# Filler products in six waits of TensorE: an attention front and two local-attention layers on one core

## Chip, core and metric

The kernel runs on one core of one Trainium2 chip. The metric is the device time of one execution in microseconds (us). A core has five engines, each with its own instruction queue, which it works off in order: TensorE (PE; its weight loads are shown apart as PEld), VectorE (DVE), ScalarE (ACT), GpSimd (POOL) and SyncE (SP), which here does nothing but issue DMA transfers. [...]

## Reference

Eight sequences of 1024 tokens, 256 wide, float32. First an attention with one head of 64 and a residual, then a normalisation over the width:

```
z = softmax(q k' * 64**-0.5 + causal mask) v;   z = z wo + bo
x = layernorm(x + z)
```

Then two layers (DEPTH = 2) of this, where `shift` moves the second half of the width by one token:

```
q, k, v = split(shift(x) wqkv)           # 8 heads of 64
q, k = rotary(l2norm(q) * q_scale), rotary(l2norm(k) * k_scale)
x = x + local_attention(q, k, v) wo      # blocks of 128 tokens: own and previous block
h = layernorm(shift(x)) * ln_g + ln_b
a, g = split(h w1 + b1)                  # 682 columns each
x = x + (a * gelu(g)) w2 + b2
```

The output is layernorm(x0 + x), with x0 the output of the front.

## The kernel before

**Products.** An operand that needs full precision is split into a high and a low half of type float32r (`halves`, L88; `split_weight`, L184), and a product takes three passes: high by high, high by low, low by high (`products`, L93, and `passes`, L135). Turning a block of 128 by 128 is also an instruction of TensorE, with an identity matrix as one operand. Every group of products writes a tile of PSUM; the tile is read by ScalarE and VectorE, and when they are done the buffer goes to a later tile. The front has 4 PSUM buffers "ps" of 128x512 and two of twice the size, "sc"; the layers have 4 and 4.

**Front** (`fronts`, L217). For each sequence b, `stages(b)` (L273) gives the steps: "load" of half a sequence; "turn" (transposes `xp` of x and split into `f_xT`; then GpSimd adds bo to x); "qkv" (`project`, L299: products `pq` of 128x512 for q and v together, `pk` for k; ScalarE and VectorE write q and k with the high half on partitions 0 to 63 and the low half on 64 to 127, and two DMA transfers, L322, make the swapped copy of q); "back" (transposes of v, `pv`); "sc" for a block of 128 queries (scores, minimum L354/L356, exponent L361/L365); "et" (transposes of the exponents); "val" (product with v, `pz`); "res" (product with wo, `py`, L410, and its sum with x, L418); "norm" (GpSimd, or VectorE for the last sequence, L428, then a DMA to `x0_d`). The table `FRONT` (L198) says in which order the steps of neighbouring sequences are emitted. Its entries "weights" (L452) take one step each of `loads` (L444): the rotary tables (`load_tables`, L470), and the weights of the first layer, which pass through two staging buffers ("stage", L466): a DMA fills the buffer, ScalarE casts the high half (L186), and VectorE or GpSimd in turn computes the low half (L189).

**Layers** (`layers`, L646). `prep` (L711) loads a pair of blocks and turns it (`l_xp`), `project_qk` (L741) makes `l_pqk` for a block and a half of the heads; the table `ORDER` (L636) and the queue of networks (`feed_forward`) set the order. `feed_forward` normalises (VectorE L964), turns the result (`m_hp`), computes `m_pag` and, through gelu, `m_pf`. The last network of the last sequence has no other work beside it.

**Order.** The program is emitted in the order of these tables; the framework's scheduler then orders each engine's queue by its own simulated times. `queued` (L114) ties TensorE's instructions of the layers to the emitted order; in the front `group["on"]` is False and nothing is tied.

## Time and profile before

| | |
|---|---|
| median of 3 runs | 2689.86 us (2679.57 to 2691.12) |
| the profiled execution | 2688.53 us, of which the span from the first to the last instruction is 2686.7 us |
| mean granted clock of TensorE | 0.986 |
| instructions | 61674, of them 22336 products and transposes |
| front (first transposes to last f_py) | 4.86 to 265.62 us |
| layers, last product | 2679.81 us |

The profile is of one execution. Its page gives the busy time of each engine; the span in 40 slices of 67 us; the chain of work that ended last, followed back from the end; and the groups of instructions. In a timeline line stand the start, the busy time, the engine, the line of the kernel, the operation and its tiles (out<-in, buffer numbers left out), how many instructions are merged in it, and in brackets how long the engine stood idle before it and what released it. In the table of windows each engine has its busy time in the stretch and, with x, its instructions; PEclk is the clock that TensorE was granted, as a share of full speed.

### The profile page before, as it was taken

How to read it: one execution, taken by the hardware profiler on the slowest of the kernel's cores; microseconds unless marked ns; L12 is line 12 of the kernel's file. 1: busy time of each engine (PE TensorE's matmuls, PEld its weight loads, DVE VectorE, ACT ScalarE, POOL GpSimd, SP SyncE). 2: the span in 40 equal slices, each digit the busy share in tenths (PEclk: the TensorE clock that was granted, in tenths of full speed). 3: DMA queues.
4: the chain of work that ended last, by engine and by line, in shares of the span. 5: the costliest groups of instructions: out<-in, count | busy, mean ns of one | idle time of the engine just before them, and what ended most of it. 6: DMA issues, size and time to landing. Idle time of an engine off the chain costs nothing.

```text
span 2686.7 us, 61674 instructions
## 1 busy us (share of the span) xinstructions
PE 2615.7 (97%) x22336; PEld 2330.3 (87%) x22336; DVE 2059.4 (77%) x6304; ACT 1721.2 (64%) x4486; POOL 1743.0 (65%) x1996
## 2 busy tenths in 40 slices
PE   7998899999999999999999999999999999999997
PEld 5776799999999999999988888988888988889887
DVE  5787677777777777777778878887787877787775
ACT  5676466666666666666676666666666666666653
POOL 4565566666666666666666776676766767667673
PEclk8999899999999999999999999999999999999998
DMA  6332211111111111111121211111111111111110
GB/s 180 99 95 72 75 35 45 45 43 41 39 35 45 45 43 42 41 33 43 45 63 51 67 52 51 41 43 50 52 50 45 39 50 52 51 44 43 47 45 25
DMA packets 147265, 141.12 MB, mean 53 GB/s; under 512 B 28808, under 2 KB 123408, under 8 KB 146960
## 3 DMA queue, kind: packets, MB, share of 16 engines
q1 hardware_dynamic: 145600, 136.72, 17.4%
q8 instruction: 176, 2.88, 0.5%
q14 instruction: 129, 1.06, 0.1%
q10 hardware_dynamic: 1360, 0.46, 0.1%
HBM read 96.74 MB, written 27.81 MB: 46 GB/s over the span
## 4 chain that ended last, share of the span: by engine, by line
PE 65%; DVE 15%; POOL 8%; ACT 6%; issue 3%; DMA 2%; SPq 0%; POOLq 0%; DVEq 0%; ACTq 0%
PE m_pag L130 16%; PE l_pqk L130 10%; PE l_po L130 8%; PE l_et L133 6%; PE m_pf L130 6%; PE l_sc L130 4%; PE l_py L130 4%; PE l_pv L130 3%; ACT l_e L703 3%; PE l_t L133 3%; DVE l_t L764 2%; POOL l_t L771 2%; DVE l_ss L757 2%; DVE ring L91 2%; POOL l_oT L915 1%
## 5 line engine op out<-in xcount | busy, mean ns | idle before, releaser
L703 ACT ACTIVATE l_e<-l_sc,l_nm 128x256 f32<-128x256 f32 (+1 forms) x992 | 456.9, 481 | 216.8 <-DVE o_mv L153 107.7
L130 PE MATMUL m_pag<-m_hT,w_h 128*128 128x256 f32 (+1 forms) x2816 | 529.4, 288 | 0.7 <-ACT m_hT L90 0.7
L771 POOL TENSOR_TENSOR l_t<-l_t,l_t 128x256 f32<-128x256 f32 x512 | 369.8, 743 | 241.5 <-DVE l_t L764 241.5
L843 DVE CUSTOM_DVE_ANT_0 l_sc<-l_sc,mask,l_nrm_y 128x256 f32<-128x256 f32 (+1 forms) x1024 | 429.1, 466 | 45.8 <-ACT l_e L703 36.9
L130 PEld LDWEIGHTS m_pag<-m_hT,w_h 128*128 128x128 f32 (+1 forms) x2816 | 433.6, 188 | 17.7 <-issue 10.6
L703 ACT ACTIVATE m_gl<-m_pag,b 128x256 f32<-128x256 f32 (+1 forms) x384 | 181.9, 474 | 348.6 <-PE m_pag L130 348.5
L130 PE MATMUL m_pag<-m_hT,w_l 128*128 128x256 f32 (+1 forms) x1408 | 395.9, 281 | 0.0
L130 PE MATMUL l_pqk<-wqk_h,l_xT 128*128 128x512 f32 x1024 | 381.7, 414 | 1.4 <-ACT l_xT L90 0.8
L144 POOL TENSOR_TENSOR l_nrm_y<-l_nrm_a,half 128x16 f32<-128x16 f32 x128 | 373.6, 2918 | 10.5
L885 ACT COPY l_eT<-l_et 128x512 f32<-128x512 f32 (+1 forms) x512 | 274.5, 565 | 144.2 <-PE l_po L130 91.4
L764 DVE TENSOR_TENSOR l_t<-l_pqk,l_tab 128x512 f32<-128x512 f32 x512 | 327.3, 681 | 0.0
L1013 DVE SCALAR_TENSOR_TENSOR m_gl<-m_pag,b,m_gl 128x256 f32<-128x256 f32 (+1 forms) x384 | 183.6, 478 | 130.2 <-ACT m_gl L703 129.9
L133 PE MATMUL l_et<-ident,l_e 128*128 128x128 f32 x1920 | 266.3, 281 | 12.6 <-DVE l_cx L733 5.4
L1017 POOL TENSOR_TENSOR m_a<-m_gl,m_a 128x256 fp32r<-128x256 f32 x320 | 233.2, 735 | 54.3 <-DVE m_a L1016 53.0
L130 PEld LDWEIGHTS m_pag<-m_hT,w_l 128*128 128x128 f32 (+1 forms) x1408 | 264.0, 188 | 0.0
L133 PEld LDWEIGHTS l_et<-ident,l_e 128*128 128x128 f32 x1920 | 211.4, 141 | 58.6 <-DVE l_cx L733 12.5
L130 PE MATMUL m_pf<-w_h,m_a 128*128 128x256 f32 x1280 | 250.3, 282 | 0.0
L757 DVE TENSOR_REDUCE l_ss<-l_sq 128x8 f32<-128x512 f32 x256 | 175.1, 684 | 86.5 <-ACT l_sq L754 82.8
L130 PE MATMUL l_po<-l_eT,l_v 128*64 128x128 f32 x3840 | 239.5, 277 | 0.0
L130 PEld LDWEIGHTS l_po<-l_eT,l_v 128*64 128x64 f32 x3840 | 208.4, 137 | 34.1 <-issue 14.1
L142 POOL TENSOR_SCALAR l_nrm_a<-l_ss 128x16 f32<-128x16 f32 x128 | 32.3, 252 | 305.2 <-DVE l_ss L757 303.7
L130 PEld LDWEIGHTS l_pqk<-wqk_h,l_xT 128*128 128x128 f32 x1024 | 194.9, 190 | 38.1 <-DVE l_on L909 1.5
(168 smaller groups left out, 6704.8 us busy)
## 6 DMA issues: line engine op xcount, KB each, us to landing
l_R<-rd_d SPq DMA_DIRECT2D x256, 128.0 KB
x<-x_d SPq DMA_DIRECT2D x96, 256.0 KB
l_tab<-tab_d SPq DMA_DIRECT2D x128, 128.0 KB
xin<-in_L_attn_x_dram SPq DMA_DIRECT2D x16, 512.0 KB
x_d<-xin SPq DMA_DIRECT2D x16, 512.0 KB
rd_d<-l_rT SPq DMA_DIRECT2D x512, 1.0 KB
x_d<-x SPq DMA_DIRECT2D x32, 256.0 KB
out_dram<-x SPq DMA_DIRECT2D x32, 256.0 KB
```

What stands on the lines that cost most here:

```text
L91: nc.vector.tensor_tensor(lo, src, hi.bitcast(FP), ALU.subtract)
L130: queued(nc.tensor.matmul(*args, **kw), part)
L133: queued(nc.tensor.transpose(*args), False)
L144: nc.gpsimd.tensor_tensor(r, a, half.to_broadcast([P, n]), ALU.pow)
L703: ins = nc.scalar.activation(*args, **kw)
L757: nc.vector.tensor_reduce(st["ss", t][:, k * HEADS : (k + 1) * HEADS], sq.rearrange("p (g d) -> p g d", d=DH), AX.X, ALU.add)
L764: nc.vector.tensor_tensor(tt[j].rearrange("p (k h d) -> p k h d", k=2, d=DH), p3, tb.unsqueeze(2).to_broadcast([P, 2, HEADS // 2, DH]), AL ...
L771: nc.gpsimd.tensor_add(a[:, :, s, :], a[:, :, s, :], bsw[:, :, 1 - s, :])
L843: nc.vector.tensor_tensor_reduce(dst, dst, mk, st["nrm", w][:, 8 * u + h : 8 * u + h + 1], BIG, ALU.add, ALU.min, nm[:, one],)
L885: nc.scalar.copy(eT[:, j, 0:m], pt[:, 0:m])
L1013: nc.vector.scalar_tensor_tensor(gl[0:z, :], a_ps, W["b1"][0:z, 0, m : m + 1], gl[0:z, :], ALU.add, ALU.mult)
L1017: nc.gpsimd.tensor_tensor(a[1], gl[0:z, :], a[0].bitcast(FP), ALU.subtract)
```

## The change

A helper `idle(dst, n)` emits n products of the identity `identr` with a new constant `wide` (the identity four times side by side, 128x512) into a PSUM tile that real work is about to write. The real work starts the tile anew, so nobody reads these products. Each filler product is tied behind TensorE's previously emitted instruction, and for this `matmul` and `transpose` note the last one in `group["prev"]`; four calls of `nc.tensor.transpose` in the front become calls of this `transpose`. The table `IDLE` has six places: before the first transposes of sequence 0 (6), before its first projection (6), before its first scores (11), before the transposes of the first `prep` of the layers (24), before its first `l_pqk` (5), and before the `m_hp` of the last network (24). The staging tag "w" of the front has 4 buffers instead of 7.

```diff
-    group = {"on": False, "in": False, "free": [], "last": None}
+    group = {"on": False, "in": False, "free": [], "last": None, "prev": None}
...
     def matmul(*args, part=False, **kw):
-        queued(nc.tensor.matmul(*args, **kw), part)
+        ins = nc.tensor.matmul(*args, **kw)
+        group["prev"] = ins.ins
+        queued(ins, part)
...
+    def idle(dst, n):
+        for _ in range(n):
+            ins = nc.tensor.matmul(dst, identr, wide, start=True, stop=True)
+            queued(ins, False)
+            if group["prev"] is not None:
+                behind(ins.ins, [group["prev"]])
+            group["prev"] = ins.ins
...
     nc.vector.tensor_copy(identr, ident)
+    wide = const.tile([P, 4 * P], FR, name="wide")
+    nc.vector.tensor_copy(
+        wide.rearrange("p (a q) -> p a q", a=4), ident.unsqueeze(1).to_broadcast([P, 4, P])
+    )
...
+    IDLE = {
+        ("turn", 0, 0, 0): 6, ("qkv", 0, 0): 6, ("sc", 0, 0): 11, ("prep", 0): 24,
+        ("qk", 0, 0): 5, ("hp", DEPTH - 1, B - 1, NT // 2 - 1): 24,
+    }
...
-            "x4": 2, "xT": 5, "q": 7, "vT": 1, "v": 5, "e": 2, "eT": 10, "w": 7,
+            "x4": 2, "xT": 5, "q": 7, "vT": 1, "v": 5, "e": 2, "eT": 10, "w": 4,
...
                     pt = ps(f"{n}_xp_{h}_{c}")
+                    idle(pt, IDLE.get(("turn", b, h, c), 0))
...
                 pq = ps(f"{n}_pq_{h}")
+                idle(pq, IDLE.get(("qkv", b, h), 0))
...
                 sc = ps_sc(f"{n}_sc_{i}").rearrange("p a q -> p (a q)")
+                idle(sc[:, 0:512], IDLE.get(("sc", b, i), 0))
...
+                px = ps(f"{n}_xp")
+                if l == 0 and b == 0:
+                    idle(px, IDLE.get(("prep", p), 0))
+                pt = px.rearrange("p (c q) -> p c q", c=2)
...
                 pqk = ps(f"{n}_pqk")
+                if l == 0 and b == 0:
+                    idle(pqk, IDLE.get(("qk", t, k), 0))
...
+            ph = ps(f"{nm0}_hp")
+            idle(ph, IDLE.get(("hp", l, b, p), 0))
+            pt = ph.rearrange("p (c q) -> p c q", c=2)
```

More of the change, by code (lines that the diff above doesn't have):

```diff
@@ L129, in matmul @@
     def matmul(*args, part=False, **kw):
-        queued(nc.tensor.matmul(*args, **kw), part)
+        ins = nc.tensor.matmul(*args, **kw)
+        group["prev"] = ins.ins
+        queued(ins, part)
     def transpose(*args):
-        queued(nc.tensor.transpose(*args), False)
+        ins = nc.tensor.transpose(*args)
+        group["prev"] = ins.ins
[3 more added lines that the diff above has]
+            ins = nc.tensor.matmul(dst, identr, wide, start=True, stop=True)
+            queued(ins, False)
+            if group["prev"] is not None:
+                behind(ins.ins, [group["prev"]])
+            group["prev"] = ins.ins
     def passes(dst, steps):
@@ L287, in turn @@
                     pt = ps(f"{n}_xp_{h}_{c}")
+                    idle(pt, IDLE.get(("turn", b, h, c), 0))
                     for j in range(TH):
-                        nc.tensor.transpose(
+                        transpose(
                             pt[:, j * P : (j + 1) * P], st["x", h][:, j, c * P : (c + 1) * P],
@@ L337, in back @@
                     t = h * TH + j
-                    nc.tensor.transpose(
+                    transpose(
                         pv[:, j, :], st["vT"][H:P, t * P : (t + 1) * P], ident[H:P, H:P]
@@ L379, in turn_e @@
                     for j in range(m):
-                        nc.tensor.transpose(
+                        transpose(
                             pt[:, j * P : (j + 1) * P], e[:, (g + j) * P : (g + j + 1) * P], ident
@@ L722, in prep @@
                         nc.vector.tensor_copy(xT[j][:, 1, 0:1], st["last"][j].bitcast(FP))
-                pt = ps(f"{n}_xp").rearrange("p (c q) -> p c q", c=2)
+                px = ps(f"{n}_xp")
+                if l == 0 and b == 0:
+                    idle(px, IDLE.get(("prep", p), 0))
+                pt = px.rearrange("p (c q) -> p c q", c=2)
                 for c in range(2):
@@ L974, in feed_forward @@
             hT = [tl("hT", [P, 2, 256], f"{nm0}_hT{j}", FR) for j in range(2)]
-            pt = ps(f"{nm0}_hp").rearrange("p (c q) -> p c q", c=2)
+            ph = ps(f"{nm0}_hp")
+            idle(ph, IDLE.get(("hp", l, b, p), 0))
+            pt = ph.rearrange("p (c q) -> p c q", c=2)
             for c in range(2):
```

## Prediction

> **What bounds the kernel now.** I read the page first: busy shares, then the slices.

> ```profile
> PE 2615.7 (97%) x22336; PEld 2330.3 (87%) x22336; DVE 2059.4 (77%) x6304; ACT 1721.2 (64%) x4486; POOL 1743.0 (65%) x1996
> ...
> PEclk8999899999999999999999999999999999999998
> ```

> TensorE is the bound, and in the layers (300 to 2600 us) it is full and at full clock; nothing that the change adds stands there. The slices below 9 are the front and the end. The windows of 1 to 5 us show where the clock was at half: 23.7 to 30.5, 54.4 to 64.7, 74.9 to 81.7, 112.5 to 115.9, about 170 to 174, 269.5 to 276.3, 286.5 to 300.2 and 2658.8 to 2669.0 us. One more is in no clock row: products stand 0.427 us apart until 16.4 us and 0.235 us from then on (starts at 12.10, 12.52, 13.38; later 17.07, 17.30, 17.77), though the column says 1.00 from the start. These two spacings are my prices of one 512-column product, at half clock and at full.

> The timeline of TensorE shows the waits that get products:

> ```profile
> 4.86 3.95 PE L289 MATMUL f_xp<-ident,xin 128*128 128x128 f32 x16 [4.86 <-DMA xin<-in_L_attn_x_dram]
> 11.08 1.22 PE L130 MATMUL f_pq<-f_xT,wqv_h 128*128 128x512 f32 x2 [2.26 <-DVE f_xT L91]
> ...
> 23.18 0.58 PE L130 MATMUL f_sc<-f_k,f_q 128*128 128x128 f32 x3 [2.99 <-DMA f_q<-f_q]
> ...
> 270.72 1.09 PE L133 MATMUL l_xp<-ident,x 128*128 128x128 f32 x4 [5.09 <-DVE xin L428]
> ...
> 2662.50 1.33 PE L133 MATMUL m_hp<-ident,m_hn 128*128 128x128 f32 x4 [6.04 <-DVE m_hn L964]
> ```

> The chain that ended last tells which of these waits the end hangs on, and through whom (start, length, what):

> ```profile
> 20.14 0.02 SPq L322
> 20.16 0.03 issue
> 20.19 2.86 DMA f_q<-f_q
> ...
> 24.17 0.76 DVE f_k L312
> ...
> 36.17 1.65 DVE f_den L369
> ...
> 46.30 0.52 ACT wqk_h L186
> ...
> 47.99 4.33 DMA st_qkv<-in_L_ffn_wqkv_dram
> ```

> Until 23 us the chain is SyncE's queue and its transfers, not TensorE; from 40 to 52 us it is the staging of layer weights, which ScalarE casts in the middle of its sequence work.

> **The change, part by part.** 76 products of 512 columns are added: 6, 6, 11, 24, 5 and 24. The instruction lists of the two programs say the rest. Layers and networks keep their order but for a few rows of the first window, so the other differences are a scheduler's reordering around sequences 0/1 and 3/4. The 7 staging buffers "w" cut to 4 cost nothing: four tiles use that tag (three weights and wo).

> *1, before the first transposes (6).* They wait for `wide`, a cast that follows identr (ends 2.13 us) on an idle VectorE; by the cast of 128x256 in the end stage (0.29 us) I call it 0.6 us. 2.7 + 6 x 0.427 = 5.3 us, 0.4 after the transposes began. The second eight wait for their own transfer (6.84), and the first eviction starts only at 9.71, behind a DMA issue of ScalarE that ends at 9.67. Cost 0.

> *2, before the first projection (6).* The list has them wait for VectorE's first f_xT, because they write the PSUM buffer that this eviction frees. That same eviction ended the 2.26 us. So they stand behind the wait, not in it: up to 6 x 0.427 = 2.6 us later, or, if the clock were already up, the 12 products that ran at half clock before save 12 x 0.192 less 6 x 0.235, 0.9 us earlier (end 19.55 before). The path hides either: the q half is ready at 15.50 and its DMA is issued at 19.53. Cost 0; 1.3 if group 3 must also run at half clock. The row speaks for that: after 16 transposes the projection still ran at 0.427.

> [...]

> *3, before the first scores (11).* 11 x 0.235 = 2.6 us in a wait of 2.99, from about 20.5. But SyncE's list now has b2, lgb and a table load ahead of the first two f_q transfers: 0.44 + 0.42 + 0.55 (their issues in its timeline) = 1.41 us later, and their 384 KB at the 211 GB/s of 20 to 25 us could add 1.8. I take +1.7 (bounds +1.4 and +3.2). In return the scores run at full clock: the chain's TensorE pieces from 23.18 to 31.99 add up to 5.94 us; by 0.235/0.427 at most 2.7 come off, I take 1.9, since latencies do not scale (bounds 0, if the clock falls in the transfer's rest, and 2.7). Also VectorE's second-half f_k (0.76 in the chain) now stands ahead of the mask work: -0.8.

> *The reordering behind it.* GpSimd adds bo to x of sequence 1 after two table products instead of before. The chain's 1.65 us f_den (usual 0.16) ran while that add did (35.44 to 37.80): -1.5. Against it, ScalarE now casts the first layer weights (L186) before it evicts the first q of sequence 1, which began at 41.11. That load was issued at 42.85; as a load of 55.39 was cast at 57.06, I put it at 45.5. So q comes about 4.6 us later, and with it v and k behind it on ScalarE. Later waits for the same weights go (1.12 before 50.5, 0.81 before 52.3: -1.9). Net +2.7; bounds -1.9 (load there in time) and +4.6. Around 140 us small bias products and w2 casts move in the same way; the chain has one 1.90 us load there: 0, bounds -1.9 and +1.9.

> *4 and 5, between front and layers (24 and 5).* Group 4 waits for VectorE's last f_py read, about 266.5 (its row ends at 266.54), and lasts 24 x 0.235 = 5.6: to 272.2, against 270.72 now, 1.5 late. Transposes at full clock take 0.65 (as at 303 us: 0.66) instead of 1.09. Group 5 ends 1.74 after their start, at 273.9; the first real product was at 272.60. The first tile's last product is the tenth: 10 x 0.235 + 0.17 gives 276.5 against 276.88. -0.4; bounds +0.8 (clock lost at once) and -1.6 (group 4 starts at 265.6). Behind it VectorE is full to 284 and GpSimd to 294.6, so the half clock of 286 to 300, which no group touches, is untouched.

> *6, the last network (24).* The list has group 6 wait for nothing that is late, so it runs from 2656.3 to 2661.9, inside the wait. The hp transposes gain 0.3 (1.33 against 1.01 in the network before). From 2664.50 to 2668.81 nineteen products ran; after the low half arrives (2665.17) seventeen at 0.118 instead of 0.213 save 1.6. All evictions of this network wait for TensorE, so it stays: -2.0. Bounds -2.6 and 0: between the last product and the first pag there are 2.2 us of transposes and evictions, in which the clock can fall again.

> How short a gap does that? These rows answer:

> ```profile
> 53.58 0.55 PE L380 MATMUL f_et<-ident,f_e 128*128 128x128 f32 x3 [1.23 <-ACT f_v L341]
> ...
> 74.37 0.66 PE L289 MATMUL f_xp<-ident,xin 128*128 128x128 f32 x4 [1.87 <-DVE f_zT L91]
> ```

> The clock fell at 54.4 and 74.9, after or within gaps of 1.23 and 1.87 us; after 1.78 (38.75) and 1.63 (2638.73) it did not. So it is near even odds in group 6. [...]

> **Sum**: 1 and 2: 0; 3: +1.7 - 1.9 - 0.8 = -1.0; reordering: -1.5 + 2.7 = +1.2; 4 and 5: -0.4; 6: -2.0. Total -2.2 us on the profiled execution's 2688.53 (span 2686.7 and 1.8 around it): 2686.3. The median of the runs is 2689.86 (2679.57 to 2691.12), 1.3 above it; the spread is larger than the sum. I say 2686.

> **Rivals.**
> *Slower: ScalarE stands at the cast.* Place: the L186 cast in front of sequence 1's q. Price: the full 4.6, and as TensorE runs out of PSUM buffers its clock falls, some 5 us at half, +2; with +3.2 on f_q and nothing regained in group 3 (-0.8 and -1.5 stay): 2688.5 + 4.6 + 2 + 3.2 - 2.3 - 2.4 = 2693.6. It decides from the point where the load lands after 43. For: in-order ScalarE, the 42.85 issue. Against: sequence 1 may be late by itself.
> *Nothing: the clock is not held.* Gaps left beside groups 3, 5 and 6 let it fall as before; the products only fill. -2.3 in VectorE, +4.4 in SyncE and ScalarE: 2690.6.
> *Faster: the half clock goes in all of the front.* If the shifted gaps also spare the stretches at 54.4 to 64.7 and 74.9 to 81.7 (17 us; 0.3 of it, as 1.9 of 6.8 in group 3, is 5) and ScalarE finds its load ready (-1.9 instead of +2.7): 2686.3 - 5 - 4.6 = 2676.7.

> **How the numbers follow.** Forecast 0.50, slower rival 0.24, nothing 0.14, faster rival 0.12. 0.5% is 13.4 us, about what a measurement of this kernel can tell from no change: 2676.4 and 2703.3. Half of the faster rival passes the first, a fifth of the slower one, with stalls in both reordered places, the second: faster 0.06, same 0.89, slower 0.05. The range takes in the faster and the slower rival's middles: 2677 to 2695.

> **What would show it.** Right: 24 products from 2656 to 2662 and pag products 0.118 apart from the first; pq still 0.43 apart behind group 2; f_q landing after 24; an l_xp start near 272. Wrong: ScalarE casting wqk_h without a wait near 41; the half clock of 54 to 65 us gone though that load is late; a difference in the layers, where I expect none.

## The result and the profile after

The changed kernel took 2692.31 us (median of 22 runs, 2685.89 to 2697.32); the kernel before took 2685.9 us beside it (22 runs, 2677.34 to 2691.17). The ratio is 1.0023 with a 95% interval of 1.0016 to 1.0031: about 6.2 us slower, between 4.3 and 8.3. I had said 2.2 us faster. The profiled execution took 2695.11 us with a span of 2693.3. A second measurement (experiment 11) gave 1.0028 (1.0017 to 1.0038).

The page of the changed kernel, engine shares and clock column:

```profile
PE 2627.8 (98%) x22412; PEld 2342.2 (87%) x22412; DVE 2057.9 (76%) x6305; ACT 1722.1 (64%) x4486; POOL 1743.8 (65%) x1996
...
PEclk8999899999999999999999999999999999999999
```

TensorE is busy 12.1 us longer, for 76 instructions more. The last slice of the clock is a 9 instead of an 8; the front's slices look as before. Its timeline at the six places (start, length; in brackets the idle time before and what ended it):

```profile
2.44 2.93 PE L143 MATMUL f_xp<-wide,identr 128*128 128x512 f32 x6 [2.44 <-DVE wide L180]
...
11.05 1.65 PE L143 MATMUL f_pq<-wide,identr 128*128 128x512 f32 x6 [2.90 <-DVE f_xT L91]
...
18.11 2.70 PE L143 MATMUL f_sc<-wide,identr 128*128 128x512 f32 x11
...
26.70 2.20 PE L130 MATMUL f_sc<-f_k,f_q 128*128 128x128 f32 x5 [5.25 <-DMA f_q<-f_q]
...
268.15 7.33 PE L143 MATMUL l_xp<-wide,identr 128*128 128x512 f32 x24 [0.97 <-DVE xin L444]
275.32 0.60 PE L135 MATMUL l_xp<-ident,x 128*128 128x128 f32 x4
...
2663.43 5.63 PE L143 MATMUL m_hp<-wide,identr 128*128 128x512 f32 x24
2669.55 0.33 PE L135 MATMUL m_hp<-ident,m_hn 128*128 128x128 f32 x1 [0.49 <-DVE m_hn L995]
...
2671.33 1.31 PE L130 MATMUL m_pag<-m_hT,w_h 128*128 128x256 f32 x4 [0.68 <-ACT m_hT L90]
```

Place 3 is over at 20.8; four transposes and one score product later TensorE waits 5.25 us for f_q (2.99 before). Place 4 lasts 7.33 us instead of 5.6, as the clock is at half from 268.88 to 272.30, and the real transposes start 4.6 us later than before (the front's last f_py product is 1.6 later too). Place 6 ends half a microsecond ahead of m_hn, and still the first pag products are 0.213 us apart from 2671.87 on.

Where the time went is read from TensorE's list, which is nearly the same in all kernels: the start of each real product, less the start of the same product in the first trace of the kernel before, as the median over a stretch. Each column gives by how much that difference grew in the stretch (us; the last column is the last network). The numbers 1 to 16 are the experiments below.

| kernel (trace) | 0-96 | 96-157 | 157-256 | 256-352 | 352-2320 | 2320-2650 | to the end |
|---|---|---|---|---|---|---|---|
| changed | -3.1 | **+9.1** | -4.5 | +0.6 | **+6.5** | -1.6 | -0.6 |
| changed again (11) | -4.4 | **+9.1** | -4.4 | +0.6 | +1.0 | 0.0 | -0.5 |
| before again (12) | -4.3 | -0.8 | -1.5 | +0.1 | -2.5 | -0.5 | 0.0 |
| nothing added (1) | +0.5 | 0.0 | 0.0 | -0.2 | -4.6 | +1.0 | +0.2 |
| products, old order (2) | -2.7 | -0.8 | +0.5 | -0.3 | +3.3 | -1.5 | -0.6 |
| new order, no products (3) | -3.7 | +7.1 | -4.5 | -0.7 | -2.8 | -0.4 | +0.2 |
| last network only (4) | -1.9 | +0.1 | -1.5 | -0.1 | -3.9 | +1.2 | -0.5 |
| 52 short (5) | -5.8 | 0.0 | -0.2 | +5.4 | +2.2 | -1.5 | +0.2 |
| code lined up (6) | -4.2 | +0.1 | -1.0 | +15.3 | -0.1 | +0.1 | -0.5 |
| first order (7) | -2.3 | +0.1 | -1.5 | +0.1 | -0.9 | +0.8 | +0.2 |
| second order (8) | -2.0 | +7.1 | -4.6 | +0.1 | -2.1 | -0.1 | 0.0 |
| 52 short in two waits (9) | -4.8 | 0.0 | +1.2 | +1.2 | +0.4 | 0.0 | +0.3 |
| last gap closed (10) | -3.3 | 0.0 | 0.0 | -0.4 | -2.1 | -0.5 | -2.0 |
| row put back (13) | -6.1 | +7.0 | -3.4 | -1.4 | -2.1 | +1.2 | +0.3 |
| one row moved (14) | -0.8 | +5.3 | 0.0 | +0.1 | -2.7 | -0.2 | 0.0 |
| second order, old TensorE list (15) | -6.5 | +9.0 | -4.6 | 0.0 | +0.5 | +1.1 | -0.3 |
| last gap closed, again (16) | -1.8 | -0.8 | -0.5 | +0.7 | -1.5 | -0.5 | -2.0 |

Three traces of one and the same TensorE list (before, 12 and 1) differ by 5 us in the first 96 us: that much is chance. What is not chance stands out: 96 to 157 in every kernel with the second reordering, and 352 to 2320, where no list was changed.

**The clock's windows.** In these traces the granted clock changes only on a grid. In the first trace of before it fell or rose at 23.71, 54.43, 74.91, 300.19 and 2669.04 us; the distances from the first are 9.00, 15.00, 81.00 and 775.00 times 3.4133 us, and between 20 and 2676 us every stretch between two changes, there and in the changed kernel's first trace, is a whole multiple of it (1 to 341 times). How much work starts in a window goes with the clock of the *next* one: in the 18 traces (20 to 2676 us, each on its own grid), all 128 windows in which products and transposes of under 1500 columns in sum started were followed by half clock, none of the 13231 with 4000 or more, and 190 of the 644 between. In the changed kernel, cut on its own grid (columns: stretch, length, busy time of PE, PEld, DVE, ACT and POOL with instructions, granted clock, DMA share, GB/s):

```profile
2665.04:2668.45 3.41, 3.41 (x17) 2.81 (x15) 1.46 (x6) 0.00 (x0) 0.75 (x3) 1.00 0.39 115
2668.45:2671.87 3.42, 2.07 (x10) 1.08 (x8) 1.68 (x5) 0.58 (x1) 2.37 (x3) 1.00 0.00 0
2671.87:2675.28 3.41, 3.31 (x16) 3.23 (x16) 0.13 (x1) 0.41 (x1) 0.87 (x1) 0.50 0.00 0
2675.28:2678.69 3.41, 3.41 (x31) 3.41 (x31) 1.98 (x5) 1.01 (x3) 1.48 (x2) 1.00 0.00 0
```

The end of the added products and the transposes fill 2.07 of the second window's 3.42 us; the third runs at half (16 instructions, then 31). The grid lies differently in the traces (a fall at 23.71 us in the first of before, at 23.12 in this one): group 2 ran at full clock in this trace (6 products in 1.65 us), but partly or wholly at half in the second one (2.26 us) and in experiment 2 (2.93 us). That can be where the spread of some 14 us between runs of one kernel comes from: of the changed kernel's 22 runs the fastest (2685.89 us) had a mean granted clock of 0.991, the slowest (2697.32) one of 0.985.

### The profile page after: what moved, and what is told of

It is laid out like the page before. It is cut to its first block, busy times and chain, and to the rows that moved or that the text cites. A ratio compares the mean times of both kernels' runs of the same rounds, so it can differ in the third digit from the quotient of the medians.

```text
span 2693.3 us, 61832 instructions
## 1 busy us (share of the span) xinstructions
PE 2627.8 (98%) x22412; PEld 2342.2 (87%) x22412; DVE 2057.9 (76%) x6305; ACT 1722.1 (64%) x4486; POOL 1743.8 (65%) x1996
## 3 DMA queue, kind: packets, MB, share of 16 engines
q14 instruction: 129, 1.06, 0.1%
## 4 chain that ended last, share of the span: by engine, by line
PE 64%; DVE 14%; POOL 8%; ACT 6%; DMA 4%; issue 3%; SPq 0%; POOLq 0%; DVEq 0%; ACTq 0%
PE m_pag L130 15%; PE l_pqk L130 10%; PE l_po L130 8%; PE m_pf L130 6%; PE l_et L135 6%; PE l_sc L130 4%; PE l_py L130 3%; ACT l_e L729 3%; PE l_pv L130 3%; PE l_t L135 3%; DVE l_t L795 2%; POOL l_t L802 2%; DVE l_ss L788 2%; DVE ring L91 2%; POOL l_oT L946 1%
## 5 line engine op out<-in xcount | busy, mean ns | idle before, releaser
L130 PE MATMUL m_pag<-m_hT,w_h 128*128 128x256 f32 (+1 forms) x2816 | 528.9, 287 | 0.8 <-ACT m_hT L90 0.7
L130 PEld LDWEIGHTS m_pag<-m_hT,w_h 128*128 128x128 f32 (+1 forms) x2816 | 432.8, 187 | 17.9 <-issue 10.6
L130 PE MATMUL m_pag<-m_hT,w_l 128*128 128x256 f32 (+1 forms) x1408 | 395.3, 281 | 0.0
L130 PE MATMUL l_pqk<-wqk_h,l_xT 128*128 128x512 f32 x1024 | 379.4, 411 | 0.6 <-DVE l_on L940 0.3
L130 PEld LDWEIGHTS m_pag<-m_hT,w_l 128*128 128x128 f32 (+1 forms) x1408 | 263.5, 187 | 0.0
L130 PE MATMUL m_pf<-w_h,m_a 128*128 128x256 f32 x1280 | 250.3, 281 | 0.0
L130 PE MATMUL l_po<-l_eT,l_v 128*64 128x128 f32 x3840 | 241.1, 278 | 0.0
L130 PEld LDWEIGHTS l_po<-l_eT,l_v 128*64 128x64 f32 x3840 | 209.9, 138 | 34.3 <-ACT m_hT L90 16.3
L130 PEld LDWEIGHTS l_pqk<-wqk_h,l_xT 128*128 128x128 f32 x1024 | 193.8, 189 | 35.7 <-DVE l_on L940 0.8
```

The lines of the kernel that those rows point to most:

```text
L130: ins = nc.tensor.matmul(*args, **kw)
```

## The experiments

"Order edges" pin one engine's list to a given order and wait for nothing. Times are medians in us. A ratio, with its 95% interval, compares with the kernel before, run beside on the same chip (medians there 2682.47 to 2684.9), and a difference in us is worked out from the ratio.

**1 to 4: order, products, tiles, last network.** Edits of the changed kernel:

```diff
 1  IDLE = {}
 2  IDLE as changed;  + pin(all engines' lists up to the first window, order of before)
 3  IDLE = {};        + pin(the same rows, order of the changed kernel)
 4  IDLE = {("hp", DEPTH - 1, B - 1, NT // 2 - 1): 24}
```

> The changed kernel with no product added: `wide` and the 4 staging buffers stay, every engine's list is that of the kernel before. In the one pair of profiles the changed kernel is 3.1 us ahead at 100 us, 5.4 behind at 155, 1.6 behind at 260, 2.2 behind at 360, and 8.7 behind at 2500: most of the loss stands in layers whose lists are the same. Theory A, the loss is the scheduler's new order in the front, and the layers' drift is chance: 2686, as before (within 2 us). Theory B, the products themselves delay: also 2686. Theory C, the other tiles (a smaller staging pool, one constant more, and so other addresses) cost in the layers: 2690 to 2692 with nothing added. Theory D, the clock's windows lie differently in every execution, and the layers' drift is that: 2686, and this kernel's profile drifts in the layers against the profile of before too, by several us.

Measured: 2684.41, ratio 1.0007 (0.9995 to 1.0019). No change clear of noise (at most 5.1 us more), and its trace loses nothing clear of chance: theory C (the tiles) isn't needed.

> All 76 added products, but the lists of all engines (up to the first layer's first window) held in the order of the kernel before by order edges without waits. Theory A (the new order costs): 2684 to 2686, the same as before or 2 us faster: f_q lands near 23, ScalarE casts wqk_h behind sequence 1's q, the last network gains 0.5. Theory B (the products cost): 2690 to 2693. Theory C (other tiles): 2690 to 2692.

Measured: 2686.81, ratio 1.0014 (1.0004 to 1.0024), +3.8 us. Neither A nor B alone: nothing is lost up to 352 us, the last network gains 0.6, but 3.3 us are lost in the layers.

> No product added, but all engines' lists held in the order of the changed kernel. Theory A: 2690 to 2693; f_q lands near 25 to 26, ScalarE waits about 5 us for wqk_h near 46, and there is a loss of 5 us or more between 130 and 155. Theory B: 2686. Theory C: 2690 to 2692.

Measured: 2687.12, ratio 1.0013 (1.0003 to 1.0023), +3.5 us. The order alone costs about half (0.8 to 6.2 us). f_q ended TensorE's wait at 26.14, ScalarE waited 6.46 us for the wqk_h load until 47.11, and 7.1 us went between 96 and 157. So order and products each cost, and 3.5 + 3.8 stands against the 6.2 of the whole.

> Only the 24 products of the last network; every list otherwise as before. My prediction: -2.0, so 2684 (pag products 0.118 us apart from the first). By the profile of the changed kernel: the clock stays up over the wait but falls for one window of 3.4 us behind the transposes (products at half clock 3.4 us instead of 4.5): -0.5, so 2685.4, not to be told from no change. Where the window's edge falls is new in every execution, so the profile may show another share of it.

Measured: 2682.04, ratio 0.9998 (0.9988 to 1.0009), no change; -0.5 in the last network, as in the changed kernel.

**5, 6 and 9: why do products lose time in layers that they don't touch?** In experiment 2, VectorE waits for the small transfer m_sh, issued at 2224.51 by SyncE. First the kernel with nothing added, then experiment 2, VectorE's timeline at the same instruction:

```profile
2225.48 0.48 DVE L166 BATCH_NORM_STATS2 m_st<-m_sh 128x6 f32<-128x128 f32 x2 [0.49 <-DMA m_sh<-x]
```

```profile
2228.67 0.49 DVE L169 BATCH_NORM_STATS2 m_st<-m_sh 128x6 f32<-128x128 f32 x2 [1.67 <-DMA m_sh<-x]
```

SyncE issues the two transfers of m_sh from 2222.50 and from 2224.51 on, in 1.65 us both times, so 2.98 and 4.16 us before these rows. The DMA queues of experiment 2 from 2226 to 2227 (packets, MB, share of the engines' time) show what else is there:

```profile
q1 hardware_dynamic: 210, 0.09, 39.8%
q8 instruction: 1, 0.02, 6.5%
```

I take the packets of queue q8 (its kind is "instruction") for TensorE's code: 176 of 16 KB in the kernel before, one for about 127 products and transposes, and 177 in the changed kernel with its 76 products more. With nothing added, this load comes at 2230, after m_sh has landed.

```diff
 5  IDLE = {("prep", 0): 52}, products of 128 columns;      + pin(order of before)
 6  IDLE as changed, but ("prep", 0): 100 of 128 columns;   + pin(order of before)
 9  IDLE = {("sc", 0, 0): 24, ("prep", 0): 28}, 128 columns; + pin(order of before)
```

> The lists of the kernel before, and only 52 short products (128 columns) ahead of the first layer, in the 5 us wait in front of l_xp: as many instructions of TensorE as places 1 to 5 add, in a place where they take no time. Theory E (new): the layers' part of the loss comes from where TensorE's code is loaded. In the second experiment a load of 16 KB of code stands in the trace at 2226 to 2227, in the middle of a small shift m_sh that VectorE then waits 1.67 us for; in the kernel with nothing added the same load comes some 5 us later in the program and hits nothing. 52 products more shift every later load by 52 of its 128 products. By E this kernel, against the profile of the kernel with nothing added, shows steps at the same places as both kernels with products do: +0.7 near 453, +1 to +3 near 1400 and near 1475, +1 near 2228, 4 to 8 us in all between 360 and 2590, and a time of 2686 to 2689 on that chip (before 2682.7). By D (only the clock's windows, chance): no step at 453 and 2228, time as with nothing added, 2683 to 2684.

Measured: 2690.13, ratio 1.003 (1.0015 to 1.0044). The steps came, but so did 5.4 us in place 4 that I had not meant: 52 products of 128 columns took 9 us there.

```profile
260.66 8.99 PE L145 MATMUL l_xp<-wide,identr 128*128 128x128 f32 x52 [0.97 <-DVE xin L448]
```

> All six places, the lists of the kernel before, but place 4 is filled with 100 products of 128 columns instead of 24 of 512 (about the same 6 us), so that 128 products stand ahead of the layers' second product instead of 52: one whole load of code. By E the layers' loads of code come where they come with nothing added, the steps at 453, 1400, 1475 and 2228 go, and the time is 2680 to 2683, 4 us or more under the second experiment's. By D or B: as the second experiment, 2686 to 2688.

Measured: 2688.63, ratio 1.0029 (1.0009 to 1.0049); the time tells nothing, since place 4 lost 15.3 us. The layers' part does: the code loads near 450, 2226 and 2302 stand where they stand with nothing added, the steps there are gone, and 352 to 2320 costs -0.1.

> The lists of the kernel before and 52 short products (128 columns, 0.107 us each at full clock, 0.21 at half) ahead of the layers, now split over two waits: 24 in place 3 (2.6 us in a wait of 3) and 28 in place 4 (3 to 4.5 us in a wait of 4 to 5). The first trial of this put all 52 into place 4, where the clock fell and they lasted 9 us, 4.7 us too long. Theory E (where TensorE's code is loaded): the front within 1 us of that with nothing added, the steps at 453, 1400, 1475, 2228 and 2304 in the layers as in the three kernels with 52 products ahead, 4 to 7 us in all; time 4 us or more over that of the kernel with nothing added, 2686 to 2690. Theory D: no steps, 2683 to 2684.

Measured: 2686.0, ratio 1.0009 (1.0 to 1.0019): +2.4 us, less than I expected, and by its time not clear of theory D. The trace is clear. Steps of TensorE's starts against the kernel with nothing added:

| us | near 450 | near 2226 | near 2302 | near 1745 | near 2596 |
|---|---|---|---|---|---|
| changed | +0.74 | +1.05 | -0.01 | +1.34 | -1.19 |
| changed again | +0.88 | +1.12 | -0.01 | +0.78 | -1.22 |
| 2: products, old order | +0.64 | +1.20 | +1.02 | -0.02 | -1.02 |
| 5: 52 short | +0.41 | +1.20 | +1.21 | -0.02 | -1.00 |
| 9: 52 short in two waits | +0.32 | +1.19 | +1.17 | 0.00 | -1.00 |
| kernels without 52 ahead (1, 3, 4, 7, 8, 10, 12 to 16, before) | up to 0.03 | up to 0.05 | up to 0.29 | up to 0.05 | -0.17 to +0.54 |
| 6: 128 ahead | +0.01 | +0.03 | +0.01 | -0.05 | -1.03 |

The steps go by where the code loads fall, which the count of TensorE's instructions shifts, not by the place or length of the added products. Near 450, 2226 and 2302 a load comes 5 to 8 us earlier in the program in the traces with the step than in those without products ahead. In the two changed kernels the load near 2302 comes 8.7 us earlier and misses m_sh: no step. Near 1328 all five traces with 52 ahead step too, by 0.39 to 1.06 us, and no other by more than 0.04. And no product is needed: near 1706 the five kernels with a new order and nothing added (3, 7, 8, 13, 15) step by 1.0 to 1.3 us, where their load comes 1 us earlier than in the others.

That the transfer lands later under a load is seen in all traces together. In the 18 traces 1028 landings of m_sh ended a wait of VectorE. The 71 under which a load of TensorE's code began, 0.25 to 1.7 us after the issue, took 2.64 to 4.72 us (median 3.27); the other 957 had a median of 2.15, and nine in ten took at most 2.33. This also explains the -1.03 of experiment 6: its load near 2596 comes 1.2 us later than in the kernels without products ahead and m_sh lands in 2.14 us instead of 3.13 to 3.70. By the same token it has a new step of +1.04 near 2262, where its load comes 3 us later and falls on m_sh. No kernel without code loads was run.

Near 1475 the starts step by 1.9 to 3 us in five traces (before, changed, 2, 5, 6), those with a window at half clock there. In three of them (changed, 2, 5) a code load also falls on a weight that ScalarE then waits 2.5 to 2.6 us for, in the other two (1.2 and 1.6 us) not; how much of this step is chance stays open.

**7, 8, 13, 14, 15: which reordering, which row?**

```diff
 7   IDLE = {};  + pin(new order for sequences 0/1, order of before behind it)
 8   IDLE = {};  + pin(order of before for sequences 0/1, new order behind it)
 13  as 8, but VectorE's w1_l<-st_w1_0_1_0_0 behind the adds to xin_3_0
 14  IDLE = {};  + pin(order of before, that one w1_l ahead of the adds)
 15  as 8, but TensorE's list as before
```

> No product added; only the first of the two reorderings (sequences 0 and 1, up to about 75 us). My prediction held this one for a loss of 1.2 (f_den -1.5, ScalarE's cast +2.7). The profiles of both kernels with the new order say a gain: 5 to 6 us behind at 45 us, but 3.1 and 3.75 ahead at 100. So 2679 to 2682 by the profiles, 2684 by my step.

Measured: 2685.12, ratio 1.0011 (1.0 to 1.0022). No change that I can tell (0 to 5.9 us). The trace is 7 to 8 us behind from 45 to 50 us and level with the others at 96.

> No product added; only the second reordering (sequences 3 and 4, about 125 to 165 us, and the few rows of the first window). My prediction: 0, bounds of 1.9 on both sides. By the two profiles with the new order it is 6.5 to 8.5 behind between 130 and 155, of which some 4 come back by 180: 2685 to 2688, a wait of TensorE before the pb1 products near 130, and half clock from there.

Measured: 2685.26, ratio 1.0018 (1.0007 to 1.0028): +4.8 us, slower as the profiles said. In the changed kernel VectorE's list shows one reason (start, length, line):

```profile
129.75 0.48 DVE L614 TENSOR_SCALAR st_w<-st_w,lgb 128x512 f32<-128x512 f32 x1
130.91 0.69 DVE L207 TENSOR_TENSOR w_l<-st_w,w_h 128x512 fp32r<-128x512 f32 x1 [0.68 <-ACT w_h L204]
131.52 0.87 DVE L444 SCALAR_TENSOR_TENSOR xin<-f_py,f_den,xin 128x256 f32<-128x256 f32 x2
```

In the kernel before the adds stand ahead of w_l:

```profile
132.78 0.48 DVE L588 TENSOR_SCALAR st_w<-st_w,lgb 128x512 f32<-128x512 f32 x1
133.17 0.87 DVE L418 SCALAR_TENSOR_TENSOR xin<-f_py,f_den,xin 128x256 f32<-128x256 f32 x2
...
134.29 0.68 DVE L189 TENSOR_TENSOR w_l<-st_w,w_h 128x512 fp32r<-128x512 f32 x1
```

VectorE waits 0.68 us for ScalarE's cast, and TensorE 1.26 us for the adds (changed kernel):

```profile
132.06 0.38 PE L436 MATMUL f_py<-woa_h,f_zT 64*128 64x256 f32 x1 [1.26 <-DVE xin L444]
```

The wait is short; what it does to the windows isn't (changed kernel, its grid):

```profile
128.93:132.35 3.42, 2.16 (x20) 1.91 (x21) 2.70 (x8) 1.36 (x3) 0.00 (x0) 1.00 0.48 142
132.35:135.76 3.41, 3.41 (x23) 2.86 (x21) 3.08 (x18) 2.65 (x11) 0.41 (x1) 0.50 0.30 77
135.76:139.17 3.41, 3.41 (x15) 3.05 (x16) 0.71 (x2) 1.11 (x2) 0.76 (x1) 0.50 0.11 28
139.17:142.59 3.42, 3.42 (x19) 3.29 (x17) 2.68 (x7) 1.57 (x4) 2.69 (x2) 0.50 0.14 38
```

Three windows at half clock, 10.2 us with TensorE busy throughout. Part of this comes back further on, where the kernel before has waits that the later TensorE is spared (0.28 us is left of them in the changed kernel):

```profile
168.76 0.66 PE L289 MATMUL f_xp<-ident,xin 128*128 128x128 f32 x4 [1.52 <-DVE f_zT L91]
170.35 1.12 PE L130 MATMUL f_pq<-f_xT,wqv_h 128*128 128x512 f32 x2 [0.93 <-DVE f_xT L91]
```

> No product added; the second reordering as in the eighth experiment, but one row of VectorE is put back: the rounding rest of a weight (w1_l, which waits for ScalarE's cast) stands behind the two residual adds of sequence 3 again (they free the PSUM that TensorE's f_py waits for), as in the kernel before. Theory F (that row makes TensorE wait, the window falls, 10 us run at half clock): between 96 and 157 us this kernel loses 0 to 2 us instead of 7 to 9, and the clock stays up from 128 to 150. If it is another row of the second order (TensorE's pb1 products ahead of f3_sc_6, the earlier w2 casts of ScalarE): 7 us as before.

Measured: 7.0 us lost all the same, in a single run (2684.15). Theory F falls as the only cause: another wait takes the place.

```profile
131.82 1.51 PE L130 MATMUL pb<-lgb,st_w 128*128 128x1 f32 x8 [1.84 <-DMA st_w<-in_L_ffn_w_dram]
```

> No product added, all lists of the kernel before, but for that one row of VectorE, which stands ahead of the two residual adds. Theory F, if the row alone is enough: a wait of TensorE of about 0.6 to 1.3 us near 132 and, where the window then falls, 5 to 9 us lost between 96 and 157. Otherwise under 1 us.

Measured: 5.3 us lost, in a single run (2690.1). The row alone is enough, through a wait of 0.64 us at 133.71 and two windows at half from 134.44.

> No product added; the second reordering on all engines but TensorE, whose list is that of the kernel before (the four pb1 products behind f3_sc_6). If TensorE's own order is the cause: 0 to 2 us lost between 96 and 157. By theory F: 7 us as in the eighth experiment.

Measured: 9.0 us lost, in a single run (2687.69). TensorE's own order is not the cause. So no single row is needed: in each of these traces another wait of 0.6 to 1.8 us stands ahead of the first window at half clock. That one of them is enough by itself is shown for the row of experiment 14 only.

**10, 11, 12, 16: the gap closed, and controls.**

```diff
 10, 16  IDLE = {("hp", ...): 24, ("pag", ...): 3}
+                pg = ps(f"{n}_pag")
+                if m == 0:
+                    idle(pg, IDLE.get(("pag", l, b, p), 0))
 11      the changed kernel          12      the kernel before
```

> The lists of the kernel before, the 24 products of the last network, and 3 more between its transposes and its first pag product. The clock's windows of 3.41 us: in the changed kernel the window with the transposes held 1536 columns of products and 512 of transposes and the next one ran at half clock. With 1536 columns more it should not fall: pag products 0.118 us apart from the first, 1.5 us less than with the 24 alone and 2 us less than before in the last 30 us, at the price of at most 0.1 for the 3 products. In the whole time: 2680 to 2682, which the spread of the runs hardly tells from no change; the profile tells. If the transposes, not the gap, let the clock fall: half clock behind them all the same.

Measured: 2680.33, ratio 0.9986 (0.9974 to 0.9998). In this trace the clock does not fall behind the transposes:

```profile
2656.70 0.59 PE L135 MATMUL m_hp<-ident,m_hn 128*128 128x128 f32 x3 [0.18 <-DVE m_hn L995]
2657.05 0.93 PE L143 MATMUL m_pag<-wide,identr 128*128 128x512 f32 x3
2657.97 1.11 PE L130 MATMUL m_pag<-m_hT,w_h 128*128 128x256 f32 x4
2658.92 0.28 PE L130 MATMUL m_pag<-m_hT,w_l 128*128 128x256 f32 x1
```

Products come 0.118 us apart from the first batch on, and the last network is 2.0 us shorter, as expected.

> The changed kernel once more, for a second profile. Theory E: the steps in the layers at 453, 1400, 1475, 2228 and 2304 are there again, because they hang on the program and not on the execution; the stretch of 130 to 155 us costs 6 us or more again; +5 to +8 in all. Theory D: the steps are elsewhere or missing.

Measured: 2691.15, ratio 1.0028 (1.0017 to 1.0038). The program's steps near 450, 1745, 2226 and 2596 and the 9.1 us between 96 and 157 are there again. Not those near 1400 (+1.3 instead of +3.2) and near 1475 (+0.5 instead of +3.0), so the layers cost +1.0 instead of +6.5. The first trace has windows at half clock there (from 1405.52 and 1484.03 us), the second has none.

> The kernel before, run as if it were a changed one: what the comparison calls no change, and a second profile of it. Expected ratio 1.000 within 0.001; in the profile no step at 453 and 2228, one of at most 2 us near 1475, where the first profile has a window at half clock.

Measured: 2682.68, ratio 0.9994 (0.9983 to 1.0006), as expected.

> The version of the tenth experiment again (24 products in the last network and 3 behind its transposes, all else as before): its ratio was 0.9986 with an interval of 0.9974 to 0.9998, while its trace shows 2.0 us in the last network and no other cause. If that is all, the ratio is 0.9993; the two together should lie clear of 1.

Measured: 2680.72, ratio 0.9985 (0.9974 to 0.9995). Clear of 1 twice: this version has the lowest ratio of the kernels run, though its intervals overlap those of experiments 4 and 12. The trace explains 2.0 of the 3.8 to 4.0 us; the rest is within the intervals.

## Why the prediction was wrong

The sum was -2.2, the measurement +6.2. By columns of the first table, the mean of the kernels with a cause less the mean of those without it: second order (changed twice, 3, 8) +8.3 and -4.1, so +4.2; places 4 and 5 (changed twice) +0.7; layers (52 ahead: changed twice, 2, 5, 9) +4.8 and -1.2 behind them; last network -0.6. That is 7.9 in all, 1.7 above the measured 6.2 and inside its interval. The first 96 us add nothing that is clear of chance.

- **"Around 140 us ... 0, bounds -1.9 and +1.9"** is the step that failed most. I had listed the moved casts and priced them by one 1.90 us load, as waits. A wait there costs the windows behind it: 8.3 us. Of these 4.1 come back: TensorE is spared the waits of 1.52 and 0.93 us near 169, and the half-clock window of 170 to 174 is gone, which alone is worth 1.5 us (157 to 256 in experiments 4, 7 and 12). Experiments 8 and 13 to 15 show the loss and also that it hangs on no single row.
- **"Full and at full clock; nothing that the change adds stands there"** (the layers) failed too. The first trace of before already has windows at half clock from 310.43, 1477.79 and 1518.75. And I compared lists, not the count of instructions: 52 more shift where code is loaded, and where a load falls on m_sh it lands about 1.1 us later (medians of 3.27 and 2.15 us). The steps near 450, 1328, 1745, 2226, 2302 and 2596 come to 2.1 to 3.0 of the 3.6 us; the rest stands near 1400 and 1475, where windows at half clock and late weights mix.
- **Place 6, -2.0**: it bought 0.5 to 0.6. The bounds (-2.6 and 0) held, the value was wrong: the gap let one window fall, as I had at even odds. With three products in the gap it is the -2.0.
- **"How short a gap does that?"** was the wrong question: behind waits of only 0.64 and 1.26 us (experiment 14, changed kernel) the clock fell too. The rows of 1.23 and 1.87 us that dropped the clock and those of 1.63 and 1.78 that didn't look contradictory as gaps; what went with the clock is how much work the window held (half clock behind all 128 windows of under 1500 columns, behind none of the 13231 with 4000 or more).
- **Place 3**: f_q, +1.7, was mis-sized: TensorE's wait ended between 25.78 and 26.70 in the four traces with the new first order (changed twice, 3, 7), between 22.69 and 23.96 in the eleven of the old order in which a wait for f_q shows, so about 3.1. The 1.9 of full clock was not won, as 5.25 us of waiting stood behind group 3.
- **ScalarE's cast, +2.7**: it waits 5.1 to 6.5 us and ends between 47.2 and 47.9, so sequence 1's q comes 6.0 later, past my 4.6. But by 96 us all is paid back: in the four traces with this order the clock is at full from about 53 to 107 us, where the first trace of before has 17 us at half (54.43 to 64.67 and 74.91 to 81.74). So the faster rival's condition came in part, and a sign that I had named for being wrong. The time of experiment 7 leaves 0 to 5.9 us open. The slower rival, which named this place, came out near the measured time by luck: this place isn't the cause.
- **Places 1 and 2, 0**: right, SyncE hides them (in the changed kernel the first q half is written at 15.59, its transfer issued at 20.96). The pq products ran at half clock for one window in three of four traces (11, 2 and 6, not the changed kernel's first), not behind all of group 2 as I had them.
- **Places 4 and 5, -0.4**: +0.7, within the bounds. Group 4 itself ran at half clock for one window and lasted 7.33 us.

Still open: which of the second order's waits matter in a given execution, and how much a code load delays other transfers than m_sh, such as the weights near 1475.

## What to carry to other kernels

Look in the trace for the grid on which the clock changes (here 3.4133 us), and cut the trace on it before filling a wait: the 24 products of the last network bought 0.5 us where the window with the transposes was left short of work (2.07 of 3.42 us), and 2.0 where three more products stood in it, so close the gap behind the transposes too. Compare the lists that a scheduler makes with and without the filler, and price a moved row by the window that its wait empties, not by the wait (here 5.3 us lost behind a wait of 0.64). And a difference of some microseconds in code that did not change can be where the instructions are loaded (here 1.05 to 1.20 us near 2226): hold the instruction count, or look for steps at the same places of several kernels.

## What the runs showed of the hardware

```profile
268.74:272.16 3.42, 3.42 (x18) 3.42 (x18) 0.00 (x0) 0.00 (x0) 0.00 (x0) 0.50 0.88 296
272.16:275.57 3.41, 3.41 (x18) 3.41 (x18) 0.00 (x0) 0.00 (x0) 0.00 (x0) 0.50 0.00 0
275.57:278.98 3.41, 3.41 (x18) 3.41 (x18) 0.00 (x0) 0.00 (x0) 0.00 (x0) 0.50 0.00 0
```

  Behind a window with eight products of 512 columns (4096 columns; changed kernel, 268.88 to 272.30) the clock was full. Behind some 16 of 128 (2048 columns) it was not. So busy time alone does not tell the next window's clock here. Columns alone don't either: in the kernel before, a window at half clock with 12 transposes of 128 columns was followed by full clock.

```profile
1518.75:1522.16 3.41, 2.88 (x14) 2.33 (x14) 3.41 (x10) 1.20 (x3) 1.70 (x4) 0.50 0.62 183
1522.16:1525.60 3.44, 2.95 (x41) 2.54 (x40) 3.32 (x6) 2.34 (x6) 3.44 (x5) 1.00 0.29 86
```

  Over the 14003 windows of the 18 traces, one border at 3250 columns parts those followed by half clock from those followed by full clock with 76 exceptions when a transposed column counts twice; counted once, the best border leaves 119, left out 185. This is a fit to these traces; why a transposed column weighs more isn't shown.
- With 52 more instructions of TensorE ahead of the layers, its starts near 2226 us, 1.9 ms later, step by 1.05 to 1.20 us in all five traces: a 16 KB load of code falls on m_sh, and VectorE goes on 4.16 us after the issue in experiment 2, 2.98 with nothing added.
